# Carrying a scan's state in place, and moving table-switching work behind other exponentials, in a four-layer state-space kernel

## Chip, cores and metric

The kernel runs on one core of a Trainium2 chip. The metric is the device time of one execution in microseconds (us). The five engines are TensorE (PE; its weight loads are shown apart as PEld), VectorE (DVE), ScalarE (ACT), GpSimd (POOL) and SyncE (SP), which here issues the DMAs. The engines run beside each other, each one its own instructions in the order in which the program lists them, and wait for each other by semaphores.

## What is computed

Eight images of 48 x 48 pixels and 96 channels pass four layers, each with a group normalisation before it and a residual sum behind it. Layers 0 and 3 are two-dimensional selective scans, layer 2 scans rows and columns, and layer 1 is an up-sampled pointwise network. The three scan layers have the same core; layer 0's is this, cut down:

```python
xz = jnp.einsum('bhwc,ec->bhwe', x, in_proj_w)
xc, z = jnp.split(xz, 2, axis=-1)                     # 192 channels each
xc = jax.nn.silu(depthwise_conv_3x3(xc) + conv_b)
xs = jnp.stack([x0, x1, x0[..., ::-1], x1[..., ::-1]], axis=1)   # rows, columns, both reversed
dts, Bs, Cs = jnp.split(jnp.einsum('bkdl,kcd->bkcl', xs, x_proj_weight), [R, R + N], axis=2)
delta = jax.nn.softplus(jnp.einsum('bkrl,kdr->bkdl', dts, dt_projs_weight) + bias)
def step(h, inp):                                      # 2304 steps, N = 16 states a channel
    u, dl, Bv, Cv = inp
    h = h * jnp.exp(dl[..., None] * A) + (dl * u)[..., None] * Bv[:, :, None, :]
    return (h, jnp.einsum('bkdn,bkn->bkd', h, Cv))
...                                                    # + D * u, the four directions summed
y = layernorm(y) * jax.nn.silu(z)
return jnp.einsum('bhwd,cd->bhwc', y, out_proj_w)
```

In layers 0 and 3 the state runs through all 2304 pixels of an image. In layer 2 every row (or column) of 48 pixels begins with a state of zero.

## The kernel before

**Blocks, slots, turns.** `scans` treats the three scan layers alike. An image and direction is cut into five blocks of rows (`BLKS`): four of 480 pixels and one of 384. A block has 192 channels x 16 states; 128 partitions hold 32 channels x 4 states at a time, so that a block is 24 *units* of one row of 480 (or 384) columns. Three units make a *slot* (8 in a block), two slots a *turn* (4 in a block, `q` from 0 to 3). A layer has 160 blocks, so the kernel has 480.

**A unit's work.** ACT computes the decay, exp(A * delta), into PSUM (`make_da`, L255), two units at a time (*a pair*, three pairs in a turn; two buffers, `ps_da`). The product of delta * u (from the tile `dd`) and B is formed into the tile `dbu` (`make_dbu`, L235), some units by DVE and some by POOL: `ON_POOL` says how many of a slot's three units POOL takes. DVE reads B from a PSUM copy that ACT makes (`copy_b`, L216), POOL from the tile `bc`, which holds a row of B and a row of C. DVE scans a pair in place (`scan`, L263). POOL multiplies three units by C in place (`make_hc`, L276), and PE sums over the states (`reduce`, L296 and L298) and adds the result to the output in PSUM.

**The state between blocks.** In layers 0 and 3 a unit has one column more than the block has pixels (481 or 385). It holds the start state: the decay is zero there, because delta is set to `FAR` (1e30), and `dbu` holds the state. Behind the scan POOL copies the last column to a small tile (`keep`, L270), and ACT copies it into the start column of the same turn of the next block (`bring`, L243). In layer 2 (`restart`) there is no such column; `FAR` stands in every row's first pixel.

**Order.** Everything is written out by hand: within a turn, the loop at the end of `scans` lists pair 0's scan, the C product of the last turn's second slot, the B product of the next turn's first slot, pair 1's exponentials, and so on. `aside` is called twice in a turn, in the middle (an even half-turn, ahead of the next turn's first pair of exponentials) and at its end (an odd one, behind that pair, ahead of its second). There the DMAs of the next block are issued, a generator `side` advances by a step (the convolution of the next image and the output stage of the last one, in layers 0 and 3), and the steps of `stage1` run, which prepare the block after the next, each at its half-turn: projection (L611), copy (L616), delta (L601, L605), Softplus (L629), delta * u on POOL (`make_du`, L422) and the stores to DRAM, from where `dd` and `bc` are read back spread over the partitions.

**ACT's functions.** Exp, Softplus and Silu stand in different tables: each Softplus or Silu among the exponentials costs one table load before it and one behind it (rows ACT_TABLE_LOAD). In layers 0 and 3 Softplus stands at half-turn 6 and the convolution's two Silus (L491, L493) at 7. In layer 2 Silu of u (L747) stands at 6, Softplus (L775) at 8 and Silu of z (L789) at 10, which are 0 and 2 of the next block. Layer 2 also has, on DVE, a gated product (L803) and an addition to the image (L818, L820) behind a projection on PE (L812).

The main loop's middle, as an instance of the order:

```python
            scan(t, 1)
            make_da(t, 2)
            copy_b(at + 3)
            make_dbu(at + 3, nc.vector)
            if t > 0:
                reduce(t - 1, 1)
            aside(at)
            bring(t + 1)
            keep(t, 0)
            make_hc(t, 0)
            make_da(t + 1, 0)
            scan(t, 2)
            copy_b(at + 4)
            finish(at + 1)
            aside(at + 1)
```

Of the kernel before, what the change touches and what calls it, by code (L numbers as in the profile page):

```python
# [26 lines left out]
WMAX = BMAX + 1  # L27
# [12 lines left out]
ON_POOL = {1: 1, 3: 2, 5: 1, 7: 2}  # L40
# [18 lines left out]
class Block:  # L59


    def __init__(self, job, k, blk, first, last, rev):
        self.job, self.k, self.blk, self.first, self.last, self.rev = job, k, blk, first, last, rev
        self.r0, self.nr = BLKS[blk]
        self.n = self.nr * SEG

    def columns(self, restart):

        self.m = self.n + (0 if restart else 1)
        self.col = None if restart else self.n if self.rev else 0  # L70
        at = 0 if restart or self.rev else 1
        self.at = slice(at, at + self.n)
# [3 lines left out]
def vss_stack_kernel(ctx: ExitStack, tc: tile.TileContext, i: dict, out: bass.AP):  # L76
# [89 lines left out]
    def scans(dirs, order, restart, a, pools, ps, stage1, opening, done, side, tail):  # L166
# [7 lines left out]

        blocks = [Block(job, k, blk, n == 0, n == len(BLKS) - 1, dirs[k][1])
# [6 lines left out]
        carry = pools["carry"].tile([P, 24], F32, tag="carry", name="carry")  # L182
        zero = pools["carry"].tile([P, 6], F32, tag="zero", name="zero")
        nc.gpsimd.memset(zero, 0.0)
# [10 lines left out]
        def load_bc(t):  # L195
# [6 lines left out]
            r = pools["bc"].tile([P, 2 * BMAX], F32, tag=f"bc{n}", name=f"bc{n}")  # L202
            rows4 = b.bcd[8 * sg:8 * sg + 8, :].rearrange("(s w) n -> s (w n)", w=2)
            nc.sync.dma_start(r[:, :2 * b.n], rows4.unsqueeze(0).to_broadcast([32, 4, 2 * b.n]))
            bcs[t] = bcs[other] = r[:, :2 * b.n].rearrange("p (w n) -> p w n", w=2)

        def copy_b(t):
# [8 lines left out]
            nc.scalar.copy(bps[t][:, :b.n], bcs[t][:, 0, :b.n])  # L216
# [4 lines left out]
        def make_dbu(t, engine):  # L221
# [4 lines left out]
            if t // 2 not in dbus:  # L226
                dbus[t // 2] = pools["dbu"].tile([P, 6 * WMAX], F32, tag="dbu", name="dbu")
# [4 lines left out]
            o = units(dbus[t // 2], b, 3 * (slot % 2) + lo, 3 * (slot % 2) + hi)[:, :, b.at]  # L232
            du = b.got[ORDER[slot][0]][:, lo:hi, 1, b.at]
            by = bps[t][:, :b.n] if engine is nc.vector else bcs[t][:, 0, :b.n]
            engine.tensor_mul(o, du, by.unsqueeze(1).to_broadcast([P, hi - lo, b.n]))  # L235

        def bring(t):
# [4 lines left out]
            o = units(dbus[t], b, 0, 6)[:, :, b.col]  # L242
            nc.scalar.copy(o, zero if b.first else carry[:, 6 * q:6 * q + 6])  # L243
# [13 lines left out]
        def scan(t, pair):  # L257
# [3 lines left out]
            if b.rev:  # L261
                da, db = da[:, ::-1], db[:, ::-1]
            nc.vector.tensor_tensor_scan(db, da, db, 0.0, ALU.mult, ALU.add)  # L263

        def keep(t, sub):
            b, q = turns[t]
            if b.last or restart:
                return
# [861 lines left out]
```

## Time and profile before

| what | value |
|---|---|
| median of 3 runs | 19436.81 us (19431.89 to 19439.07) |
| the profiled execution: its own time | 19445.46 us |
| its span | 19443.7 us |
| DVE, POOL, PE, ACT busy | 16830.2, 16019.2, 15206.3, 14190.2 us |
| first scan layer, 130 to 5940 us: DVE, POOL busy | 5433.9, 5306.3 of 5810 us |
| pointwise layer, 5940 to 7373 us: DVE, POOL busy | 296.4, 20.2 of 1433 us |
| row layer, 7373 to 13490 us: DVE, POOL busy | 5624.9, 5356.0 of 6117 us |
| last scan layer, 13613 to 19426 us: DVE, POOL busy | 5433.9, 5306.5 of 5813 us |
| table loads on ACT, at L255 | 986 of 1283 ns each |
| DMA engines' mean busy share | 0.47 in the scan layers, 0.42 in the row layer |

The page gives, for each group of instructions, its line, engine, shapes and count, then its busy time and the mean duration of one, then the idle time of the engine just ahead of such instructions and what ended it. "<-ACT ps_da L255" behind an idle time means that the instruction started when ACT's line 255 had written `ps_da`. A group's mean mixes shapes where it says "+3 forms". In a timeline each row has its start, its duration, the engine and line, and in brackets the idle time ahead of it. Two neighbours' durations can overlap by some 0.08 us.

### The profile page before, as it was taken

What the parts mean: (1) busy time and instruction counts of PE and PEld (TensorE: products, weight loads), DVE (VectorE), ACT (ScalarE), POOL (GpSimd) and SP (SyncE); (2) the same over time, 40 slices, a digit from 0 to 9 for tenths busy, and PEclk for the clock granted to TensorE, in tenths of its full rate; (3) what the DMA queues carried; (4) which work ended last, traced back from release to release, by engine and by line L of the source; (5) the groups of instructions that cost most, each with busy time, mean ns of one, the idle gap of its engine ahead of it and who ended that gap; (6) DMA issues with size and microseconds to landing.
All of it is one profiled execution on the core that took longest, in us unless ns stands there. A gap on an engine that the chain in (4) does not pass through costs nothing.

```text
span 19443.7 us, 172969 instructions
## 1 busy us (share of the span) xinstructions
PE 15206.3 (78%) x53500; PEld 4384.0 (23%) x53500; DVE 16830.2 (87%) x11289; ACT 14190.2 (73%) x22262; POOL 16019.2 (82%) x9825
## 2 busy tenths in 40 slices
PE   6777777777777897888888988887777777777776
PEld 1211211211114562222222222222121121121121
DVE  7999999999993228999999999997999999999998
ACT  6777877877872227788788787786778778778776
POOL 6999999999991007888888888886999999999998
PEclk6776776776767777888888878878677677677675
DMA  4444444444443324444434444443444444444444
GB/s 135 162 159 162 160 159 162 159 161 161 156 165 60 49 43 147 145 142 151 149 141 147 147 143 146 147 145 119 158 162 159 160 162 160 157 162 161 157 162 138
DMA packets 768487, 2829.45 MB, mean 146 GB/s; under 512 B 235724, under 2 KB 298668, under 8 KB 640926
## 3 DMA queue, kind: packets, MB, share of 16 engines
q1 hardware_dynamic: 767558, 2818.38, 44.1%
q8 instruction: 422, 6.91, 0.1%
q14 instruction: 507, 4.15, 0.1%
HBM read 2371.42 MB, written 446.69 MB: 145 GB/s over the span
## 4 chain that ended last, share of the span: by engine, by line
DVE 32%; PE 19%; POOL 16%; ACT 15%; issue 13%; DMA 5%; SPq 0%; POOLq 0%; DVEq 0%; ACTq 0%
DVE dbu L263 20%; POOL dbu L276 12%; DVE dbu L235 11%; ACT ps_da L255 4%; PE ps_s L740 3%; ACT L255 3%; PE ps_y L296 3%; DMA dd<-dd 2%; PE ps_h L970 2%; POOL dds L422 2%; PE ps_s L611 2%; PE ps_y L983 2%; PE ps_s L812 1%; POOL dbu L235 1%; PE ps_side L482 1%
## 5 line engine op out<-in xcount | busy, mean ns | idle before, releaser
L263 DVE TENSOR_TENSOR_SCAN dbu<-ps_da,dbu 128x962 f32<-128x962 f32 (+3 forms) x5760 | 11853.3, 2070 | 927.4 <-ACT ps_da L255 925.1
L276 POOL TENSOR_TENSOR dbu<-dbu,bc 128x1440 f32<-128x1440 f32 (+1 forms) x3840 | 11433.5, 2984 | 1051.2 <-DVE dbu L263 837.5
L255 ACT ACTIVATE ps_da<-dd,w_l_a 128x481 f32<-128x481 f32 (+3 forms) x11520 | 7414.9, 648 | 2754.7 <-DVE dbu L263 2548.7
L296 PE MATMUL ps_y<-dbu,w_red 128*32 128x480 f32 (+1 forms) x23040 | 4947.0, 747 | 2996.0 <-POOL dbu L276 2991.6
L298 PE MATMUL ps_y<-dbu,w_red 128*32 128x480 f32 (+1 forms) x7680 | 4906.1, 747 | 0.0
L235 DVE TENSOR_TENSOR dbu<-dd,ps_b 128x1440 f32<-128x1440 f32 (+5 forms) x3840 | 4641.3, 1209 | 261.3 <-ACT ps_b L216 217.7
L235 POOL TENSOR_TENSOR dbu<-dd,bc 128x480 f32<-128x480 f32 (+3 forms) x1920 | 3023.4, 1575 | 58.8 <-DMA bc<-bcd 35.5
L296 PEld LDWEIGHTS ps_y<-dbu,w_red 128*32 128x32 f32 x23040 | 743.6, 125 | 6938.7 <-POOL dbu L276 5185.4
L216 ACT COPY ps_b<-bc 128x480 f32<-128x480 f32 (+1 forms) x3360 | 1798.8, 535 | 298.9 <-DVE dbu L235 270.1
L740 PE MATMUL ps_s<-xpad,w_l_cw 128*128 128x480 f32 (+1 forms) x2560 | 1760.7, 840 | 2.3 <-ACT xpad L124 1.6
L482 PE MATMUL ps_side<-xpad,w_l_cw 128*128 128x480 f32 (+1 forms) x2880 | 1652.6, 703 | 4.5 <-ACT xpad L124 4.5
L255 ACT ACT_TABLE_LOAD x986 | 1265.0, 1283 | 17.5
L113 POOL MEMSET w_l_cw<- 128x1760 f32 (+1 forms) x3 | 5.8, 1941 | 1346.3 <-DVE x L950 1340.9
L422 POOL TENSOR_TENSOR dds<-dds,u 96x480 f32<-96x480 f32 (+1 forms) x640 | 791.9, 1237 | 202.9 <-ACT dds L629 202.9
L601 PE MATMUL ps_s<-bcl,dtw 6*96 6x480 f32 (+1 forms) x1280 | 880.6, 777 | 90.7 <-ACT dds L605 80.9
L611 PE MATMUL ps_s<-u,w_l_xp 96*38 96x480 f32 (+1 forms) x1280 | 931.7, 867 | 2.8 <-ACT dds L605 1.5
L270 POOL COPY carry<-dbu 128x3 f32<-128x3 f32 x2048 | 382.5, 187 | 635.0 <-DVE dbu L263 628.5
L292 PE MATMUL ps_y<-ysum,w_ident 96*96 96x480 f32 (+1 forms) x960 | 747.5, 868 | 114.1 <-ACT ysum L652 112.6
L482 PEld LDWEIGHTS ps_side<-xpad,w_l_cw 128*128 128x128 f32 x2880 | 581.1, 227 | 1130.4 <-issue 940.9
L740 PEld LDWEIGHTS ps_s<-xpad,w_l_cw 128*128 128x128 f32 x2560 | 531.8, 213 | 1096.4 <-issue 961.9
L298 PEld LDWEIGHTS ps_y<-dbu,w_red 128*32 128x32 f32 x7680 | 683.1, 125 | 0.0
L768 PE MATMUL ps_s<-bcl,dtw 6*96 6x480 f32 (+1 forms) x640 | 424.1, 799 | 181.7 <-ACT bcl L762 181.7
(146 smaller groups left out, 12660.7 us busy)
## 6 DMA issues: line engine op xcount, KB each, us to landing
dd<-dd SPq DMA_DIRECT2D x512, 1443.0 KB
bc<-bcd SPq DMA_DIRECT2D x1536, 480.0 KB
dd<-dd SPq DMA_DIRECT2D x256, 1440.0 KB
dd<-dds SPq DMA_DIRECT2D x512, 360.8 KB
dd<-dd SPq DMA_DIRECT2D x128, 1155.0 KB
bc<-bcd SPq DMA_DIRECT2D x384, 384.0 KB
dd<-dds SPq DMA_DIRECT2D x256, 360.0 KB
dd<-dd SPq DMA_DIRECT2D x64, 1152.0 KB
```

Source lines behind the costliest of these rows:

```text
L216: nc.scalar.copy(bps[t][:, :b.n], bcs[t][:, 0, :b.n])
L235: engine.tensor_mul(o, du, by.unsqueeze(1).to_broadcast([P, hi - lo, b.n]))
L255: nc.scalar.activation(da[:, at:at + b.m], b.got[half][:, u % 3, 0, :], AF.Exp, scale=a[:, b.k, ci:ci + 1])
L263: nc.vector.tensor_tensor_scan(db, da, db, 0.0, ALU.mult, ALU.add)
L276: nc.gpsimd.tensor_mul(h, h, bcs.pop(2 * t + sub)[:, 1, :n].unsqueeze(1).to_broadcast([P, 3, n]))
L296: nc.tensor.matmul(y[32 * g:32 * g + 32, :n], lhsT=wc["red"][:, :32], rhs=hc[:, g, b.at], start=False, stop=(slot == 3))
L298: nc.tensor.matmul(y[DH:, :n], lhsT=wc["red"][:, 32:], rhs=hc[:, 2, b.at], start=(slot == 0), stop=(slot == 3))
L422: nc.gpsimd.tensor_mul(rows(du, n), rows(dt, n), u)
L482: nc.tensor.matmul(pu[:, :n], lhsT=flat[:, at:at + P], rhs=xpad[:, r0 + dy:r0 + dy + nr, dx:dx + W], start=(tap == 0), stop=(tap == 8))
L601: nc.tensor.matmul(got["p"][:DH, :n], lhsT=dtw[2 * NS:, b.k, half, :], rhs=b.bcl[2 * NS:, :n], start=True, stop=True)
L611: nc.tensor.matmul(got["p"][:NBC, :n], lhsT=w[f"{l}_xp"][:, b.k, half, :], rhs=u[:, half], start=(half == 0), stop=(half == 1))
L740: nc.tensor.matmul(got["u", half][:, :n], lhsT=flat[:, at:at + P], rhs=shifted(off), start=(tap == 0), stop=(tap == 3))
```

## The change

The unit of layers 0 and 3 grows to two extra columns, one at each end (482 or 386). `FAR` stands in the one where the scan comes in (`came`), zero in the other (`goes`), so that the scan itself copies its last state into the far column. The odd blocks of an image are held mirrored, and so are scanned in the other direction: the far column of one block is the start column of the next, and the four turns of a block have four fixed tiles (`rooms`), in which the state stays. `keep` and `bring` go. `begin` sets the start column to zero at an image's first block, and moves it where the block's length changes. The inputs and outputs of mirrored blocks are read and written through reversed views (`view`). The tile `bc` gets a leading column, so that B is read with its neighbours, and the rows of B and C start one column later.

POOL takes two units in slots 1, 5 and 7 and one in slot 3 (it was one in 1 and 5, two in 3 and 7): seven of a block's 24, where it was six.

In layers 0 and 3 Softplus moves from half-turn 6 to 7, both delta * u products stand at 8, and the convolution of the next image starts with a shorter first piece, so that its Silus fall on half-turn 3. In layer 2 the steps of `stage1` move one half-turn ahead, Silu to 5, Softplus to 7, Silu of z to 9; the copy of L762 stands apart from the matmuls ahead of it. In `aside` the steps behind a finished output (`later`) run ahead of `stage1`'s.

```diff
-WMAX = BMAX + 1
+WMAX = BMAX + 2
-ON_POOL = {1: 1, 3: 2, 5: 1, 7: 2}
+ON_POOL = {1: 2, 3: 1, 5: 2, 7: 2}
...
     def columns(self, restart):
-        self.m = self.n + (0 if restart else 1)
-        self.col = None if restart else self.n if self.rev else 0
-        at = 0 if restart or self.rev else 1
-        self.at = slice(at, at + self.n)
+        self.mirrored = not restart and self.blk % 2 == 1
+        self.back = self.rev != self.mirrored
+        if restart:
+            self.m = self.n
+            self.at = self.by = slice(0, self.n)
+            return
+        self.m = self.n + 2
+        self.at = slice(1, self.n + 1)
+        self.came, self.goes = (self.m - 1, 0) if self.back else (0, self.m - 1)
+        self.by = slice(0, self.n + 1) if self.back else slice(1, self.n + 2)
+
+    def view(self, t, col):
+        v = seq(t, col)
+        if len(v.shape) == 3:
+            v = v[:, self.r0:self.r0 + self.nr, :]
+            return v[:, ::-1, ::-1] if self.mirrored else v
+        v = v[:, :, self.r0:self.r0 + self.nr, :]
+        return v[:, :, ::-1, ::-1] if self.mirrored else v
...
-            nc.sync.dma_start(r[:, :2 * b.n], rows4.unsqueeze(0).to_broadcast([32, 4, 2 * b.n]))
+            nc.sync.dma_start(r[:, 1:1 + 2 * b.n], rows4.unsqueeze(0).to_broadcast([32, 4, 2 * b.n]))
+            lead = b.at.start
+            bcs[t] = bcs[other] = r[:, 1 - lead:1 - lead + b.m], r[:, 1 + b.n:1 + 2 * b.n]
...
-            nc.scalar.copy(bps[t][:, :b.n], bcs[t][:, 0, :b.n])
+            nc.scalar.copy(bps[t][:, :b.m], bcs[t][0])
...
-        def bring(t):
+        def begin(t):
             if t >= nt or restart:
                 return
             b, q = turns[t]
-            o = units(dbus[t], b, 0, 6)[:, :, b.col]
-            nc.scalar.copy(o, zero if b.first else carry[:, 6 * q:6 * q + 6])
+            o = units(rooms[q], b, 0, 6)[:, :, b.came]
+            if b.first:
+                nc.gpsimd.memset(o, 0.0)
+            elif blocks[t // (NG // 2) - 1].m != b.m:
+                c = blocks[t // (NG // 2) - 1]
+                nc.gpsimd.tensor_copy(o[:, 1:], units(rooms[q], c, 1, 6)[:, :, c.goes])
...
             next(beside, None)
-            run(at)
             for step in later.pop(at, []):
                 step()
+            run(at)
...
-            if b.rev:
+            if b.back:
                 da, db = da[:, ::-1], db[:, ::-1]
...
-                keep(t - 1, 1)
...
-            bring(t + 1)
-            keep(t, 0)
+            begin(t + 2)
...
-                        yield
+                        if not brief or slot in (2, 4, 6):
+                            yield
...
-            return {0: s0, 1: s1, 3: s3, 4: s4, 5: lambda: biased(1), 6: s6, 7: du(0), 8: du(1),
+            return {0: s0, 1: s1, 3: s3, 4: s4, 5: lambda: biased(1), 7: s6, 8: du,
                     NG + 1: store(0), NG + 2: store(1)}
...
-            return {3: conv(0), 4: conv(1), 6: s2s3, 7: s5, 8: s6, 9: s7, 10: s8, 11: lambda: store_dd(b, 1)}
+            return {2: conv(0), 3: conv(1), 5: s2, 6: s5, 7: s6, 8: s7, 9: s8, 10: lambda: store_dd(b, 1)}
```

## The prediction

> **What bounds the kernel now.** I read the page from the top: busy shares first, then the groups, then the waits, and last the timeline of one block, because the shares alone do not say which engine another engine's gain would reach.
>
> ```profile
> PE 15206.3 (78%) x53500; PEld 4384.0 (23%) x53500; DVE 16830.2 (87%) x11289; ACT 14190.2 (73%) x22262; POOL 16019.2 (82%) x9825
> ...
> L263 DVE TENSOR_TENSOR_SCAN dbu<-ps_da,dbu 128x962 f32<-128x962 f32 (+3 forms) x5760 | 11853.3, 2070 | 927.4 <-ACT ps_da L255 925.1
> L276 POOL TENSOR_TENSOR dbu<-dbu,bc 128x1440 f32<-128x1440 f32 (+1 forms) x3840 | 11433.5, 2984 | 1051.2 <-DVE dbu L263 837.5
> L270 POOL COPY carry<-dbu 128x3 f32<-128x3 f32 x2048 | 382.5, 187 | 635.0 <-DVE dbu L263 628.5
> ```
>
> DVE leads, POOL is close behind. The busy time by stretch says it more sharply: in the first scan layer (130 to 5940 us) DVE is busy 5433.9 of 5810 us and POOL 5306.3; in the row layer (7373 to 13490) 5624.9 and 5356.0 of 6117; the last scan layer repeats the first. The waits by engine say that POOL mostly waits for the scans (about 390 us in each scan layer, 666 in the row layer), and that DVE, where it is idle, mostly waits for exponentials: 310.9, 293.1 and 310.9 us in the three layers. So DVE sets the pace, and 925 us of its idle time have one releaser. The row layer has another 151 us of DVE waiting for PE (L820, L818, L803).
>
> The timelines of DVE and of ACT around one block border show where the 925 us arise.
>
> ```profile
> 3010.14 2.15 DVE L263 TENSOR_TENSOR_SCAN dbu<-ps_da,dbu 128x962 f32<-128x962 f32 x1
> 3012.83 2.16 DVE L263 TENSOR_TENSOR_SCAN dbu<-ps_da,dbu 128x962 f32<-128x962 f32 x1 [0.53 <-ACT ps_da L255]
> 3014.90 1.63 DVE L235 TENSOR_TENSOR dbu<-dd,ps_b 128x1440 f32<-128x1440 f32 x1
> 3018.25 2.16 DVE L263 TENSOR_TENSOR_SCAN dbu<-ps_da,dbu 128x962 f32<-128x962 f32 x1 [1.72 <-ACT ps_da L255]
> ...
> 3024.99 1.63 DVE L235 TENSOR_TENSOR dbu<-dd,ps_b 128x1440 f32<-128x1440 f32 x1
> 3026.54 2.15 DVE L263 TENSOR_TENSOR_SCAN dbu<-ps_da,dbu 128x962 f32<-128x962 f32 x1
> ```
>
> ```profile
> 3007.72 1.28 ACT L629 ACT_TABLE_LOAD   x1
> 3009.02 1.01 ACT L629 ACTIVATE dds<-dds 96x960 f32<-96x960 f32 x1
> 3009.93 0.18 ACT L243 COPY dbu<-zero 128x6 f32<-128x6 f32 x1
> 3010.13 1.28 ACT L255 ACT_TABLE_LOAD   x1
> 3011.43 1.37 ACT L255 ACTIVATE ps_da<-dd,w_l_a 128x481 f32<-128x481 f32 x2
> 3012.73 0.54 ACT L216 COPY ps_b<-bc 128x480 f32<-128x480 f32 x1
> 3013.29 1.28 ACT L491 ACT_TABLE_LOAD   x1
> ```
>
> The Softplus burst (3007.72 to 3011.43, two table loads) makes the next turn's first pair of exponentials 0.53 us late. The Silu burst of the convolution comes only one copy later, and makes the second pair 1.72 us late: ACT had no time to recover. I sorted the idle time before each of a block's 12 scans by its place. In a scan layer it is 107 us before scan 0 (Softplus), 135 before scan 1 (Silu, in about half of the blocks), 59 before scan 4, 12 elsewhere. In the row layer: 174 before scan 0 (Silu), 115 before scan 3 (Softplus), 8 elsewhere.
>
> **The change part by part.**
>
> 1. *Bursts behind the first pair.* A turn that nothing disturbs gives the slack. From the end of a turn's first scan, DVE needs 1.55 us (three-unit product, 3024.99 to 3026.54) + 2.07 (scan) + 0.54 or 1.05 (one- or two-unit product) + 2.07 until it wants the next turn's first pair, and 2.07 + 1.55 more until it wants the second. Before: ACT finishes its pair and copy 2.2 us after that point, a Softplus burst takes 3.71, a pair 1.36: ready at 7.3, wanted at 6.74, so 0.55 late, which the trace shows as 0.53. After: the first pair can start when scan 1 ends (3.62) and ends at 5.05, the copy at 5.6, the burst (3.5 without the copy of L243) at 9.1, the second pair at 10.5. It is wanted at 9.83, since the fourth turn now has the one-unit product. So Softplus still costs DVE about 0.7 us; by the same sum with the durations of the 384-column blocks (1.75 us a scan, 0.58 an exponential) 1.3. **The stall moves, it does not go**: 128 x 0.7 + 32 x 1.3 is about 130 us a layer, where it was 107. What goes is the collision: Silu now stands in the second turn by itself and costs the same 0.7 or 1.2, for 75 bursts (150 loads at L491 in two layers) about 60 us, where it was 135.
>
> 2. *Scan 4's wait* comes from the copy of L616, which waits for PE L611, which stands behind the reduction of POOL's last product of the block. The du product that stood ahead of that product on POOL (L422, 1.28 us) moves behind it, and the first turn's DVE product grows by a unit (0.5 us of slack). I take 59 down to 10 us; between 0 and 59. Per scan layer, then, 313 becomes 130 + 60 + 10 + 12 = 212, so -101, and -202 for both.
>
> 3. *Row layer.* All three bursts move to odd half-turns. Softplus (3.6 us) in the fourth turn: 130 us as above. Silu of u in the third turn has the gated product (0.6 us, L803) on DVE beside it: about 15. Silu of z in the first turn has that and a two-unit product: 0. With 8 elsewhere 153, where it was 297: -144. A new wait is added here: the Softplus load now comes half a turn after its matmuls of L768, not a full turn. They follow POOL's product and its reduction, ready by my sums about 1 us early; behind the load stand only exponentials, and DVE pays what comes late.
>
> 4. *One product unit in 24 goes from DVE to POOL.* DVE's rows by shape: 1129 ns for two units, 628 for one, 0.50 us a block; the short blocks 0.40. 384 x 0.50 + 96 x 0.40 = **231 us off DVE**, on the path while DVE is the bound. POOL pays 2.115 - 1.151 = 0.96 us a block by the same rows. Whether it can is the question of the next point. The "GPSIMD Engine Reference" of the Trainium skill (section Engine selection) speaks against this part: elementwise products belong on VectorE, GpSimd being about twice as slow. The rows agree on the price, 0.96 against 0.50. By that rule alone the kernel would lose 0.46 x 480, about 220 us; by the rows it wins as long as POOL keeps idle time.
>
> 5. *POOL's ledger.* The trace has a pattern: L276 takes 3.24 us in the row layer, but 2.90 or 3.07 in the scan layers, by the columns at which its three units start in their tile. A unit costs 1.08 where its own operand starts at column 0 or 1 modulo 4, and 0.91 at 2 or 3; this fits all shapes, and L422 and L235 too. After, two units lie 482 apart from column 1, so the scan layers get 2.90 and 3.07 alternately (now 3.07 throughout in the reversed directions), and their two-unit products of L235 become about 1.88, from 2.06. POOL's occupied time for an image, small gaps left out, is 666 us in a scan layer, DVE's 682, of 727. POOL after: about +6 (product units) - 6 (L276) + 2 (du) - 10 (the carry copies: 187 ns each, but the product behind follows so closely that only 0.08 us is won) + 2 = 660; DVE 673. Row layer: POOL 673 + 23 = 696, DVE 706 - 10 = 696. So POOL does not become the bound in the scan layers, and draws level in the row layer. But in all layers the rows of B and C now start at an odd column, which no row shows. If only the distance between the operands counts, the row layer's L276 drops to 2.73, 4 us a block off POOL; if odd starts cost all units the slow rate, it is 3.24 everywhere; the nearest row above that is L422 reading with a step, 1.44 for 480 columns. I take no effect, since odd starts of the other operand cost nothing extra.
>
> 6. *The rest.* The copies of L243 (1024 x 0.19 us) leave ACT, which has spare time; in the bursts they are counted above. Scans grow by two columns: by the slope between the 770 and 962 rows 4 ns, 3840 times, +16 us; the 960 and 962 rows differ by nothing, so 0 to 16. The few memsets and copies of the new start columns (512 on POOL, about 0.1 us) lie in POOL's spare time. Mirrored reads and writes have no row; contiguous and stepped rows (L652: 0.55 and 0.97, L611: 0.57 to 0.99) bound them, on engines with slack. In the row layer DVE's saved half microsecond in the second turn partly turns into waiting for the projection (L820 waits 74 times already): +40 us, between 0 and 77.
>
> Sum: -202 - 144 - 231 + 16 + 40 = **-521 us**. The profiled execution took 19445.46 us (span 19443.7), 8.7 above the median of 19436.81, so 18,924 by the profile's own time and about **18,915** as a median.
>
> The table loads deserve one more look. In the trace a load takes 1.28 us and the next instruction follows 0.02 us later. "ScalarE: Activation LUTs" of the Trainium skill (What ACT_TABLE_LOAD costs) adds a drain of about 1.4 us to each switch. By that page a burst would be some 2.8 us longer and this placement would stall DVE in every turn with a burst; the rows do not show the drain.
>
> **The rivals.**
>
> - *The bursts vanish altogether* (17%). For: POOL's and PE's lag shrink too, and a DVE slightly late at one place finds ACT ready at the next. Against: the slack sum above, which fits the old stall within 0.05 us. All remaining waits of 153 + 2 x 212 us gone gives 18,340; half of them 18,630. Range 18,350 to 18,750.
> - *Stalls only move, and POOL draws level everywhere* (13%): L276 at the slow rate in all layers. POOL's image in a scan layer is then 660 + 39 = 699, level with DVE and its stalls, and only point 4 is won, and partly: 19,437 - 231 + 56 = 19,260. Range 19,080 to 19,390.
> - *Slower* (12%): POOL becomes the bound because reading B and C from an odd column costs like a stepped read. POOL has 727 - 660 = 67 us an image to give, 19.2 full blocks with 8 products each: it decides from 0.43 us more per product, 3.4 us at L276. At 3.6 POOL needs 755 us an image in a scan layer, 28 more than now, 16 times, and 751 in the row layer, 15 fewer, 8 times: about 19,760. At 1.44 a unit (4.3 us) it would be above 21,500. For it: no row has this operand odd. Against: the other operand starts odd already without extra cost.
> - *It does not do what it says* (3%): within 0.2% of before. The order of the built program shows each burst directly behind a first pair and its copy, so this needs gains and losses to cancel.
>
> **How the numbers follow.** The forecast (18,760 to 19,080 by itself) has 55%. The 80% range runs from the middle of the first rival to the second's: 18,550 to 19,300. Faster by over 0.2% (39 us, about what a measurement here can tell from no change): 55 + 17 + 13 = 85%; within 0.2%: 3%; slower: 12%.
>
> **What would show it.** L263's wait for ACT falls from 925 to about 560 to 590 us, none of it before scan 0, most before scan 1; L235 on DVE loses 231 us, the same line on POOL gains at most some 400; carry lines are gone; L276's groups show 2.90 and 3.07 in the scan layers. Wrong would be: L276 above 3.4 us, DVE waiting for POOL at the scans, the gated products or the row layer's additions waiting longer for PE than 150 us more, or a scan wait above 800 us.

## The result, and the profile after

The changed kernel takes 19445.32 us (median of 12 runs, 19425.83 to 19452.23), the kernel before 19433.89 us beside it: a ratio of 1.0005, 95% interval 0.9996 to 1.0014. The forecast was 18,915 us. Nothing was won, although the copies are gone and the two busiest engines have less to do.

The page's engine line and the two costliest groups of the changed kernel (L289 is the scan, L295 the C product) stand against the first lines shown of before; carry copies no longer exist:

```profile
PE 15106.2 (78%) x53500; PEld 4344.8 (22%) x53500; DVE 16588.6 (85%) x11289; ACT 14003.6 (72%) x20977; POOL 15119.7 (78%) x8304
...
L289 DVE TENSOR_TENSOR_SCAN dbu<-ps_da,dbu 128x964 f32<-128x964 f32 (+3 forms) x5760 | 11820.8, 2069 | 846.0 <-ACT ps_da L281 844.6
L295 POOL TENSOR_TENSOR dbu<-dbu,bc 128x1440 f32<-128x1440 f32 (+1 forms) x3840 | 10670.3, 2796 | 2543.1 <-DVE dbu L289 2532.9 <-POOL dbu L295 0.4
```

DVE has 242 us less to do and POOL 900 us less, and the span is the same: both only wait more. The waits by engine of the changed kernel (in total, times, longest, in us) say where DVE does; L817 is the row layer's gated product:

```profile
DVE dbu L289 <- ACT ps_da L281: 844.6, 751, 4.2
DVE gated L817 <- PE ps_y L317: 499.7, 89, 8.9
...
DVE dbu L257 <- DMA dd<-dd: 83.9, 36, 4.4
```

The first was to fall to 560 to 590 us and has fallen by 81. The other two in before:

```profile
DVE dbu L235 <- DMA dd<-dd: 42.8, 29, 2.8
...
DVE gated L803 <- PE ps_y L298: 35.2, 56, 6.4
```

Two of the forecast's own signs of being wrong are there: the gated product waits 464 us longer for PE (the mark was 150), and a scan wait stands above 800 us.

From each trace I took the time between a layer's first scan and the first scan of its last block, which splits the zero into three parts. Kernels whose scan layers are alike (after, e1, e2, e3, e7) agree there within 8 us; from the first scan of scan layer 0's last block to the first of the row layer, mostly the pointwise layer, which no kernel changes, it is 1448 to 1483 us, so that small differences are better read by layer than in the total. The table has all kernels of this study; a ratio is to the runs of before on the same chip (their medians are 19,429 to 19,440 us):

| kernel | time, us | ratio to before, 95% interval | scan layer 0 | row layer | scan layer 3 |
|---|---|---|---|---|---|
| before | 19433.89 | 1 | 5771.4 | 6078.3 | 5774.5 |
| after | 19445.32 | 1.0005 [0.9996, 1.0014] | 5657.3 | 6313.9 | 5664.4 |
| e1_old_row_steps | 19098.01 | 0.9832 [0.9817, 0.9846] | 5659.0 | 5982.8 | 5660.7 |
| e2_conv1_back | 19375.44 | 0.9975 [0.9965, 0.9984] | 5662.5 | 6245.1 | 5657.7 |
| e3_softplus_back | 19513.91 | 1.0044 [1.0030, 1.0059] | 5655.2 | 6392.2 | 5658.8 |
| e4_units_back | 19464.63 | 1.0017 [1.0007, 1.0026] | 5680.3 | 6286.5 | 5681.3 |
| e5_scan_bursts_only | 19350.98 | 0.9952 [0.9937, 0.9966] | 5729.1 | 6073.2 | 5726.2 |
| e6_in_place_only | 19244.77 | 0.9900 [0.9885, 0.9915] | 5725.1 | 5984.6 | 5726.6 |
| e7_conv_by_rows | 19117.85 | 0.9832 [0.9813, 0.9852] | 5660.0 | 5983.2 | 5661.9 |
| e8_units_by_layer | 19079.15 | 0.9811 [0.9794, 0.9827] | 5649.6 | 5954.3 | 5648.7 |
| e9_bc_one_later | 19373.60 | 0.9968 [0.9956, 0.9981] | 5785.5 | 5997.7 | 5783.2 |
| e10_bc_three_later | 19392.74 | 0.9977 [0.9967, 0.9986] | 5749.1 | 6070.7 | 5750.1 |
| e11_second_dds | 19451.38 | 1.0008 [0.9999, 1.0017] | 5783.0 | 6082.3 | 5787.4 |
| e12_best_second_dds | 19167.00 | 0.9865 [0.9852, 0.9879] | 5700.3 | 5952.8 | 5702.4 |

The scan layers won 114 and 110 us, the row layer lost 236. The forecast had about -170 for each scan layer and -180 for the row layer, so the miss is first of all there.

**The stall in the row layer.** A block of the changed kernel in a column direction, in the timelines of DVE, PE and POOL:

```profile
10122.38 2.17 DVE L289 TENSOR_TENSOR_SCAN dbu<-ps_da,dbu 128x960 f32<-128x960 f32 x1
10128.66 0.65 DVE L817 TENSOR_TENSOR gated<-zb,ps_y 96x480 f32<-96x480 f32 x1 [4.11 <-PE ps_y L317]
```

```profile
10112.33 2.50 PE L826 MATMUL ps_s<-gated,wo 96*96 96x480 f32 x4
10114.67 12.18 PE L763 MATMUL ps_s<-xpad,w_l_cw 128*128 128x384 f32 x16
10126.78 0.60 PE L315 MATMUL ps_y<-dbu,w_red 128*32 128x480 f32 x3
```

```profile
10112.83 5.42 POOL L295 TENSOR_TENSOR dbu<-dbu,bc 128x1440 f32<-128x1440 f32 x2 [1.64 <-DVE dbu L289]
```

POOL had both C products of a turn done at 10118.25. Their reductions (L315, L317) stand in PE's queue behind the convolution of the block after the next (L763, 16 records in one piece, 12.18 us), and begin at 10126.78. The gated product waits for the last of them, DVE 4.11 us. This convolution is of a block of 384 pixels; for 480 pixels the 16 records take 15.18 us. For 384 pixels in a row direction they take 5.33 us, and DVE does not wait:

```profile
9719.60 5.33 PE L763 MATMUL ps_s<-xpad,w_l_cw 128*128 128x384 f32 x16
```

In the row layer's old order, half-turns 3 and 4, the two reductions stand between the convolution's halves; in the new, 2 and 3, nothing does.

A second stall comes with Softplus. ACT, DVE and PE of the changed kernel, around the new place of Softplus (L789):

```profile
9697.93 0.54 ACT L238 COPY ps_b<-bc 128x480 f32<-128x480 f32 x1
9701.76 1.28 ACT L789 ACT_TABLE_LOAD   x1 [3.29 <-issue]
9703.06 1.20 ACT L789 ACTIVATE dds<-ps_s,w_l_dtb 96x480 f32<-96x480 f32 x2
9704.28 1.28 ACT L281 ACT_TABLE_LOAD   x1
9705.58 2.64 ACT L281 ACTIVATE ps_da<-dd,w_l_a 128x480 f32<-128x480 f32 x4
```

```profile
9701.17 1.63 DVE L257 TENSOR_TENSOR dbu<-dd,ps_b 128x1440 f32<-128x1440 f32 x1
9706.97 2.16 DVE L289 TENSOR_TENSOR_SCAN dbu<-ps_da,dbu 128x960 f32<-128x960 f32 x1 [4.17 <-ACT ps_da L281]
```

```profile
9699.78 3.51 PE L782 MATMUL ps_s<-bcl,dtw 6*96 6x480 f32 x4
```

ACT stands 3.29 us in front of the load, in the trace under "issue", that is without a releaser. That it waits for the matmuls that Softplus reads (L782, begun at 9699.78) is inferred from the times. Idle ahead of scan 1 is 1.80 us a block on average, 286 us for the layer; that of ACT ahead of these loads is 124.2 us (62 of the 160 wait, up to 3.3 us).

### The profile page after: what moved, and what is told of

The parts are those of the page before. It is cut to its first block, busy times and chain, and to the rows that moved or that the text cites. A ratio compares the mean times of both kernels' runs of the same rounds, so it can differ in the third digit from the quotient of the medians.

```text
span 19446.5 us, 169763 instructions
## 1 busy us (share of the span) xinstructions
PE 15106.2 (78%) x53500; PEld 4344.8 (22%) x53500; DVE 16588.6 (85%) x11289; ACT 14003.6 (72%) x20977; POOL 15119.7 (78%) x8304
## 4 chain that ended last, share of the span: by engine, by line
DVE 34%; PE 23%; ACT 19%; issue 14%; DMA 6%; POOL 4%; SPq 0%; DVEq 0%; ACTq 0%; POOLq 0%
DVE dbu L289 22%; DVE dbu L257 10%; ACT ps_da L281 6%; PE ps_s L763 6%; PE ps_y L315 4%; ACT L281 4%; POOL dbu L295 3%; DMA dd<-dds 2%; PE ps_h L984 2%; PE ps_y L311 2%; ACT ps_b L238 2%; PE ps_y L997 2%; PE ps_side L502 1%; ACT L651 1%; DMA dd<-dd 1%
## 5 line engine op out<-in xcount | busy, mean ns | idle before, releaser
L295 POOL TENSOR_TENSOR dbu<-dbu,bc 128x1440 f32<-128x1440 f32 (+1 forms) x3840 | 10670.3, 2796 | 2543.1 <-DVE dbu L289 2532.9
L289 DVE TENSOR_TENSOR_SCAN dbu<-ps_da,dbu 128x964 f32<-128x964 f32 (+3 forms) x5760 | 11820.8, 2069 | 846.0 <-ACT ps_da L281 844.6
L281 ACT ACTIVATE ps_da<-dd,w_l_a 128x482 f32<-128x482 f32 (+3 forms) x11520 | 7391.9, 648 | 2920.0 <-DVE dbu L289 2701.0
L315 PE MATMUL ps_y<-dbu,w_red 128*32 128x480 f32 (+1 forms) x23040 | 5091.0, 776 | 2019.3 <-POOL dbu L295 2016.5
L317 PE MATMUL ps_y<-dbu,w_red 128*32 128x480 f32 (+1 forms) x7680 | 5051.9, 776 | 0.0
L257 DVE TENSOR_TENSOR dbu<-dd,ps_b 128x1443 f32<-128x1443 f32 (+10 forms) x3840 | 4410.2, 1148 | 307.3 <-ACT ps_b L238 218.9
L257 POOL TENSOR_TENSOR dbu<-dd,bc 128x962 f32<-128x962 f32 (+6 forms) x1920 | 3104.4, 1617 | 105.3 <-DMA bc<-bcd 72.3
L315 PEld LDWEIGHTS ps_y<-dbu,w_red 128*32 128x32 f32 x23040 | 811.9, 130 | 6081.6 <-POOL dbu L295 4353.9
L238 ACT COPY ps_b<-bc 128x482 f32<-128x482 f32 (+3 forms) x3360 | 1793.0, 534 | 248.6 <-DVE dbu L257 214.9
L763 PE MATMUL ps_s<-xpad,w_l_cw 128*128 128x480 f32 (+1 forms) x2560 | 1683.6, 819 | 7.5 <-DVE x L834 5.4
L623 PE MATMUL ps_s<-bcl,dtw 6*96 6x480 f32 (+1 forms) x1280 | 945.1, 830 | 753.3 <-ACT z L515 557.0
L311 PE MATMUL ps_y<-ub,diag 96*96 96x480 f32 (+1 forms) x640 | 513.9, 900 | 499.6 <-DVE gated L817 499.6
L763 PEld LDWEIGHTS ps_s<-xpad,w_l_cw 128*128 128x128 f32 x2560 | 512.5, 201 | 1075.8 <-issue 971.3
L317 PEld LDWEIGHTS ps_y<-dbu,w_red 128*32 128x32 f32 x7680 | 749.3, 131 | 0.0
L817 DVE TENSOR_TENSOR gated<-zb,ps_y 96x480 f32<-96x480 f32 (+1 forms) x320 | 195.3, 610 | 499.7 <-PE ps_y L317 499.7
```

Source lines behind the costliest of these rows:

```text
L238: nc.scalar.copy(bps[t][:, :b.m], bcs[t][0])
L281: nc.scalar.activation(da[:, at:at + b.m], b.got[half][:, u % 3, 0, :], AF.Exp, scale=a[:, b.k, ci:ci + 1])
L295: nc.gpsimd.tensor_mul(h, h, bcs.pop(2 * t + sub)[1].unsqueeze(1).to_broadcast([P, 3, n]))
L311: nc.tensor.matmul(ys[b, half][:DH, :n], lhsT=lhsT, rhs=rhs, start=True, stop=False)
L315: nc.tensor.matmul(y[32 * g:32 * g + 32, :n], lhsT=wc["red"][:, :32], rhs=hc[:, g, b.at], start=False, stop=(slot == 3))
L317: nc.tensor.matmul(y[DH:, :n], lhsT=wc["red"][:, 32:], rhs=hc[:, 2, b.at], start=(slot == 0), stop=(slot == 3))
```

## Experiments

First the theory: the row layer's steps cost what the rest wins, because PE's queue is in their way. Its rivals: the unit that went to POOL, the odd column, or mirrored reads cost it.

**e1, the row layer's steps put back**, all else as changed.

```diff
+            run(at)
             for step in later.pop(at, []):
                 step()
-            run(at)
...
-            return {2: conv(0), 3: conv(1), 5: s2, 6: s5, 7: s6, 8: s7, 9: s8, 10: lambda: store_dd(b, 1)}
+            return {3: conv(0), 4: conv(1), 6: s2, 7: s5, 8: s6, 9: s7, 10: s8, 11: lambda: store_dd(b, 1)}
...
-                for _ in range(3 * NG + 3):
+                for _ in range(3 * NG + 4):
```

> The changed kernel with the row layer's steps back at their old half-turns (convolution 3 and 4, Silu 6, Softplus 8, Silu of z 10, and the steps behind a finished output after them); all else stays changed. Theory A: the row layer lost 236 us by its moved steps alone: the convolution's eight matmuls now stand ahead of two reductions in PE's queue (the gated product waits 500 us for PE, where it was 35), and Softplus stands too close behind its matmuls. Then the gated wait returns to about 35 us, the row layer takes 6030 to 6080 us instead of about 6310, and the kernel about 19,150 to 19,200. Theory B: PE was already the hidden bound of the row layer, and what DVE saves there comes back as waits for PE whatever the steps: then the row layer stays above 6200 us and the kernel above 19,350.

19098.01 us, below what was expected: the row layer loses 331 us, the scan layers stay. So the moved steps alone cost 331 us, where -144 were forecast, and the unit, the odd column and the mirrored reads, which e1 keeps, do not cost it. Its waits:

```profile
DVE dbu L289 <- ACT ps_da L281: 837.7, 822, 3.6
DVE gated L817 <- PE ps_y L317: 25.3, 27, 5.4
```

**e2, only the convolution's second half put back** to half-turn 4, so that the reductions pass between.

```diff
-            return {2: conv(0), 3: conv(1), 5: s2, ...
+            return {2: conv(0), 4: conv(1), 5: s2, ...
```

> The changed kernel with only the second half of the row layer's convolution back at half-turn 4, so that it stands behind the reductions of the turn's first half in PE's queue. Theory A: the gated wait for PE falls from 500 us to under 100, Silu of u waits for PE by 1 to 3 us in the 80 column blocks instead, and about 200 to 350 us of the kernel's time go: 19,100 to 19,250. Theory B (PE is the bound anyway): the gated wait falls, but the same time comes back in the waits before the scans, and the kernel stays within 60 us of 19,445.

```profile
DVE dbu L289 <- ACT ps_da L281: 1256.6, 832, 7.4
```

The gated wait is gone (21.1 us), but only 69 us of time in the row layer, where 200 to 350 were expected; the whole lies between the ranges of the two theories. Silu of u at half-turn 5 (L770) now waits 421.7 us for the convolution's end (267.3 in the changed kernel), with the exponentials behind it, and idle ahead of scan 10 goes from 0.19 to 2.97 us a block. One queue was relieved, the next has the same matmuls in its way.

**e3, only Softplus put back** to half-turn 8, with Silu of z still at 9.

```diff
-            return {..., 7: s6, 8: s7, 9: s8, ...
+            return {..., 8: lambda: (s6(), s7()), 9: s8, ...
...
-                for _ in range(3 * NG + 3):
+                for _ in range(3 * NG + 1):
```

> The changed kernel with only the row layer's Softplus back at half-turn 8, ahead of Silu of z at 9 (the normalisation of the next image starts two half-turns earlier, which its PSUM buffer needs). Theory A: the 286 us of waiting before a block's second scan go, since Softplus no longer follows its own matmuls; but Silu of z comes one copy behind it, the collision that the scan layers had before: 0.5 us before scan 3 and up to 1.7 before scan 4, 100 to 300 us in 160 blocks. The gated wait of 500 us stays. So 19,350 to 19,450. Theory B: no wait for Softplus's matmuls was in it, the 286 us are the burst's own length, and they stay or only change their place: 19,440 to 19,550.

Idle ahead of scan 1 is gone, as theory A said, but 1.41 us a block stand ahead of scan 4, where two bursts now follow each other, and the gated wait grows to 567.8 us. The row layer is 78 us longer, so the time lies in theory B's range: the waiting mostly changed its place.

**e7, the convolution reads by rows in all directions**, order as changed. In the column directions that is another input than the layer's: e7 leaves out the transposed reading and serves to measure alone.

```diff
-                                         rhs=shifted(off), start=(tap == 0), stop=(tap == 3))
+                                         rhs=flatly(off), start=(tap == 0), stop=(tap == 3))
```

> The changed kernel, but the row layer's convolution reads the image by rows in the two column directions as well (another input for these directions; all else as in the changed kernel). Theory A: what stands ahead of the reductions is the length of the eight matmuls when they read down a column, about 12 us where they take 5 in the row directions: the gated product's wait for PE falls from 500 us to under 60, and the row layer from about 6310 to about 5900, the kernel to about 19,000 to 19,100. Theory B: the order on PE alone is at fault, whatever the length: the gated wait stays above 200 us.

```profile
DVE dbu L289 <- ACT ps_da L281: 1009.7, 834, 4.2
DVE gated L820 <- PE ps_y L317: 7.6, 10, 5.4
```

The convolution's records in after, then in e7:

```profile
L763 PE MATMUL ps_s<-xpad,w_l_cw 128*128 128x480 f32 (+1 forms) x2560 | 1683.6, 819 | 7.5 <-DVE x L834 5.4 <-ACT xpad L142 1.6 <-ACT zb L803 0.5
```

```profile
L766 PE MATMUL ps_s<-xpad,w_l_cw 128*128 128x480 f32 (+1 forms) x2560 | 1028.5, 551 | 9.9 <-DVE x L837 6.9 <-ACT xpad L142 1.6 <-ACT zb L806 0.7
```

With the order untouched and only the duration of the same matmuls changed (a mean of 551 ns for 819), the gated wait goes and the row layer loses 331 us. e1 keeps the length and changes the order, e7 the reverse, and the gated wait goes in both: the long form at this place in PE's queue is its cause. That both win the same time is partly chance, for e7 still has Softplus coming late (2.56 us a block ahead of scan 1, where e1 has none). The kernel's 19117.85 us lie just above the expected range.

**e4, POOL's units put back**, all else as changed.

```diff
-ON_POOL = {1: 2, 3: 1, 5: 2, 7: 2}
+ON_POOL = {1: 1, 3: 2, 5: 1, 7: 2}
```

> The changed kernel with POOL's share of the products as before (one unit in slots 1 and 5, two in 3 and 7). Theory A: DVE is the bound in both scan layers and gets 0.5 us a block back: +77 us in each; in the row layer, where DVE waits for PE at the gated product, most of it is hidden: 0 to +77. So 19,600 to 19,680. Theory B: POOL or PE bounds the scan layers now, and the kernel stays within 60 us of 19,445.

The unit is worth 23 and 17 us in the scan layers, and minus 27 in the row layer with its new steps; 77 each were forecast. The time lies in theory B's range, but not for its reason: in the first scan layer of the changed kernel POOL waits 457 us for scans. Occupied time of DVE for an image of a scan layer goes from 673 back to 683 us, but its idle time falls from 38 to 30. By place, idle ahead of scan 1 is 0.43 us a block with the old units and 0.75 with the new, ahead of scan 7 0.24 and 0.46: the work was taken out of the turns in which a burst of ACT needs cover.

**e5 and e6, single parts on the kernel before.** e5 has the scan layers' moved bursts alone (conv's shorter first piece, Softplus at 7, both du at 8), e6 the state in place alone, with its tiles and the leading column of `bc`.

> The kernel before with one part of the change: in the two scan layers Softplus at half-turn 7, both delta * u products at 8, the convolution's Silus at 3. States, units and row layer as before. Theory A: it is this part that won the scan layers' time, since the two bursts of one block border no longer collide: each scan layer loses 50 to 90 us of its 5771 (first scan of the first block to the first scan of the last), so 19,260 to 19,340. Theory B: the scan layers' gain of 114 us each comes from the unit moved to POOL and from the copies that went, and the bursts only change their place: 19,400 to 19,450.

> The changed kernel with all steps and POOL's share of the units as before: only the states are carried in place. Theory A: the copies were hidden on POOL and ACT, so that alone this part wins little: ACT's 0.2 us in each Softplus burst, 0 to 30 us a scan layer; nothing in the row layer although POOL's products there fall from 3.24 to 2.73 us, as POOL does not bound it. 19,370 to 19,440. Theory B: POOL's shorter queue (carry copies gone, product 0.5 us shorter in the row layer) shortens what PE and DVE wait for: 19,250 to 19,350.

The bursts are worth 42 and 48 us in the scan layers, a little less than the 50 to 90 expected. The state in place is worth 46 and 48 there (0 to 30 expected), and, unforeseen, 94 us in the row layer, in which no state is carried. For a scan layer the three parts give 42 + 46 + 23 = 111, and 114 were measured. In the row layer -94 and the +331 of the steps give 237, and 236 were measured.

In e5, idle ahead of scans falls by 81 us a layer. A part returns as a wait that before did not have in this layer: DVE waits 49 us for `dd`. Over all layers, in the waits of e5:

```profile
ACT dds L607 <- DMA dd<-dds: 202.1, 125, 14.1
...
DVE dbu L235 <- DMA dd<-dd: 133.8, 120, 4.3
```

It was 31.3 and 42.8 us. The stores of `dds` now stand on SP's queue waiting for the later Softplus (1742.4 us in e5, 363.0 in before), and the loads behind them start later.

**e9 and e10: the kernel before, with B and C one or three columns later** in the tile `bc`.

```diff
-            r = pools["bc"].tile([P, 2 * BMAX], F32, tag=f"bc{n}", name=f"bc{n}")
+            r = pools["bc"].tile([P, 1 + 2 * BMAX], F32, tag=f"bc{n}", name=f"bc{n}")
...
-            nc.sync.dma_start(r[:, :2 * b.n], rows4.unsqueeze(0).to_broadcast([32, 4, 2 * b.n]))
+            nc.sync.dma_start(r[:, 1:1 + 2 * b.n], rows4.unsqueeze(0).to_broadcast([32, 4, 2 * b.n]))
```

> The kernel before with one edit: the rows of B and C start at column 1 of the tile bc, not at 0, in all layers. Distance theory: what a unit of a POOL product costs hangs on how far its two operands' start columns lie apart, modulo 4 (0.91 us at 2 or 3, 1.08 at 0 or 1). Then L276 takes 2.73 us in the row layer (now 3.24), and in the scan layers 3.07 in three of four cases and 2.90 in one, as now but in other blocks; the row layer loses about the 94 us that the kernel with the in-place state alone lost there, from 6078 to about 5985, the scan layers stay at 5771 within 10, and the whole is about 19,340 us, 0.995. Rival, the fixed tiles for the scans or the memsets brought the 94 us in that kernel: L276 may change, but the row layer stays within 20 us of 6078, ratio 1.000. Rival, any odd column costs: L276 slower somewhere and the time above 1.000.

> The same edit with column 3 in place of 1. Distance theory: in the row layer the operands lie 1 apart modulo 4, so L276 stays at 3.24 us and the row layer at 6078 within 15; in the scan layers L276 takes 2.90 us in three of four cases and 3.07 in one (now the reverse), 0.68 us a block off POOL, which by the row layer's rate (94 us of time for 640 of POOL) is about 15 us a layer; the whole about 19,405 us, 0.998 to 0.999. Rival, an odd start of B and C is what makes it fast: L276 takes 2.73 us in the row layer as with column 1, and the row layer loses some 90 us.

L276 within the row layer (7450 to 13300 us), by shape, of before, of e9 and of e10 (busy, mean in ns, idle):

```profile
L276 POOL TENSOR_TENSOR dbu<-dbu,bc 128x1440 f32<-128x1440 f32 x975 | 3146.6, 3243 | 504.5 <-DVE dbu L263 459.7 <-DMA bc<-bcd 44.2
```

```profile
L276 POOL TENSOR_TENSOR dbu<-dbu,bc 128x1440 f32<-128x1440 f32 x985 | 2688.7, 2735 | 1041.4 <-DVE dbu L263 973.4 <-DMA bc<-bcd 68.0
```

```profile
L276 POOL TENSOR_TENSOR dbu<-dbu,bc 128x1440 f32<-128x1440 f32 x970 | 3132.6, 3245 | 494.0 <-DVE dbu L263 457.2 <-DMA bc<-bcd 36.1
```

One column makes the product 0.51 us shorter, three columns do nothing: it is the distance, not the odd start, and not the fixed tiles, which e9 does not have. The scan layers answer too: their full products take 3.07, 3.07, 3.07 and 2.91 us in e9, 2.91, 2.90, 3.08 and 2.91 in e10, each of the eight as the distances say. In time, e9 wins 81 us in the row layer, of the 94 of e6, and loses 14 and 9 in the scan layers, which I had at 0 within 10; e10 wins 22 and 24 there.

**e8, the fastest: e1 with POOL's units chosen by layer**, three of them in slot 7, so that DVE and the copy of B skip it.

```diff
-ON_POOL = {1: 2, 3: 1, 5: 2, 7: 2}
+ON_POOL = {False: {1: 1, 3: 2, 5: 1, 7: 3}, True: {1: 1, 3: 1, 5: 2, 7: 3}}
...
+            if ON_POOL[restart].get(slot) == 3:
+                return
```

> The changed kernel with the row layer's old steps, and seven units a block on POOL as in the change, but in other slots: those whose turn has no burst give a unit, those with a burst keep it on DVE, where it is the slack that hides part of the burst (scan layers: one unit of slots 1 and 5, two of 3, three of 7; row layer: one of 1 and 3, two of 5, three of 7). Theory A: a unit taken from DVE in a turn with a burst wins nothing, since DVE then waits as much longer for the exponentials; in a turn without, it wins its 0.5 us. So the scan layers lose another 50 us each and the row layer 80 against 19,098: 18,880 to 18,960. Theory B: a unit's place does not matter, only DVE's total: 19,070 to 19,130.

19079.15 us, 9 and 12 us less than e1 in the scan layers and 28 in the row layer, with as many units on POOL. It beats both kernels; beside e1 the intervals overlap. Idle ahead of scan 1 is 0.44 us a block in the scan layers, for e1's 0.75, so the place decides where DVE waits. In time theory A failed by its sizes (50 and 80 us), and the whole lies in theory B's range: of the 51 us less of waiting ahead of scans in the first scan layer, 12 come back as waiting for `dd` and 25 as busy time of DVE itself, whose cause stays open.

**e11 and e12, a second buffer for `dds`**, in e5 and in e8. The room came from the output stage: two small tiles share a buffer, the input tile `xi` has one for two.

```diff
-                 "carry": pool("carry", 1), "dds": pool("dds", 1), "bcl": pool("bcl", 1),
+                 "carry": pool("carry", 1), "dds": pool("dds", dds), "bcl": pool("bcl", 1),
...
-        wt, big, zp, lnp, xio = pool("wt", 1), pool("big", 3), pool("z", 1), pool("ln", 2), pool("xio", 2)
+        wt, big, zp, lnp, xio = pool("wt", 1), pool("big", 3), pool("z", 1), pool("ln", 2), pool("xio", 1)
```

> The kernel before with the scan layers' bursts moved alone (19,350.98 us; its scan layers 5729.1 and 5726.2 us, idle ahead of scan 7 about 0.33 us a block, ScalarE's line 607 waiting 202 us for the store of dds) and, in layers 0 and 3, a second buffer for the tile dds; to make room, two small tiles of the output stage share a buffer and its input tile has one buffer instead of two. Theory: behind the moved steps the store of dds starts later, so ScalarE's next write to dds waits for it to land, with the exponentials queued behind. Then that wait goes to near 0, the idle ahead of scan 7 falls below 0.1, each scan layer loses 30 to 45 us (about 5690), and the whole is about 19,270 us; VectorE's wait for dd (134 us) stays, since the store and the load behind it are as late as before. Rival: the idle ahead of scan 7 is the Silu burst itself, moved; then the wait for dds goes and the scan layers stay at 5729 within 10 us. Rival: the shared tiles of the output stage cost as much as the second buffer wins; then the waits of the lines behind xi and sq grow by 30 us or more a layer.

> The same second buffer for dds in the fastest kernel so far (the changed kernel with the row layer's old steps and POOL's units chosen by layer: 19,079.15 us, scan layers 5649.6 and 5648.7). Theory of the store: idle ahead of scan 7 (0.24 us a block) and part of that ahead of scan 4 go, each scan layer 20 to 40 us shorter, the whole about 19,020 us, 0.978 to 0.980 of before. Rival, the Silu burst itself: 19,079 within 15 us.

My theory fell. ACT's wait for the store of `dds` is gone, yet idle ahead of scan 7 stays (0.32 us in e11, 0.33 in e5): that is the Silu burst, in its new place. Ahead of scan 9 it falls from 0.20 to 0.06, so that was the store. And each scan layer becomes longer, by 54 and 61 us in e11, 51 and 54 in e12: with one buffer the load of `xi` waits on SP's queue for the store of the last, with the loads of `dd` behind it. That was the second rival. SP's waits in the first scan layer of e11, then DVE's in all layers:

```profile
SPq L535 <- DMA x<-xi: 164.1, 28, 10.2
```

```profile
DVE dbu L235 <- DMA dd<-dd: 280.1, 121, 9.9
```

The second buffer's own worth is left open: no kernel here has it beside two of `xi`.

## Why the prediction was wrong, point by point

The sum of the forecast beside what single parts were worth: bursts in the scan layers (points 1 and 2) -202, measured -90; the row layer's steps (3) -144, measured +331; the unit (4) -231, measured -40 in the scan layers and -2 in the row layer with its old steps; the state in place (6) +16, measured -188, of which 94 in the row layer; DVE's waiting for the projection (6) +40, gone in the changed kernel. That is +11 for -521.

- **Point 3 is the step that failed**: the row layer, -144 forecast, +331 measured (after against e1). It costed the bursts that move and the Softplus matmuls, and left out what else moves: the convolution's 16 records on PE, which at half-turns 2 and 3 stand in one piece ahead of two reductions. Half of the directions read down the columns and need 12.18 to 15.18 us there. This gave the gated wait of 499.7 us, and e7 shows that it is the convolution's length. The second part, "ready by my sums about 1 us early", was wrong in sign: 62 of the 160 loads wait, up to 3.3 us, 124.2 us in all, and idle ahead of scan 1 is 286 us for the 130 of the sum. What point 3 had right: the bursts ahead of scans 0 and 3 are gone (0.02 and 0.00 us a block for 1.09 and 0.72), and the row additions' wait for PE fell from 116 to 2 us, where point 6 feared 40 more.
- **Point 1** was right in mechanism, and for the waits nearly in size. A Softplus burst behind the first pair of the changed kernel, in ACT's and DVE's timelines:

```profile
3030.26 1.28 ACT L651 ACT_TABLE_LOAD   x1
3031.56 1.01 ACT L651 ACTIVATE dds<-dds 96x960 f32<-96x960 f32 x1
3032.58 1.28 ACT L281 ACT_TABLE_LOAD   x1
```

```profile
3033.10 1.62 DVE L257 TENSOR_TENSOR dbu<-dd,ps_b 128x1443 f32<-128x1443 f32 x1
3035.28 2.17 DVE L289 TENSOR_TENSOR_SCAN dbu<-ps_da,dbu 128x964 f32<-128x964 f32 x1 [0.56 <-ACT ps_da L281]
```

  The second pair is 0.56 us late for the 0.7 of the sum (here a step of the output stage stands ahead of the burst on ACT and one on DVE); the layer's mean ahead of scan 1 is 0.75, 120 us for 130. Silu, ahead of scan 7, costs 0.46, 73 us for 60. As in before, no drain stands behind a load.
- **Point 2**: 59 us ahead of scan 4 were to fall to 10 and fell to 39. The copy behind the projection still waits for PE (L638, 2.69 us at 3042.01). With point 1, a layer's idle ahead of scans was to be 212 us and is 258. Beside this came DVE's wait for `dd`, 43 us in the first scan layer: the moved stores on SP, which the sum had not followed, as it had not followed the convolution on PE.
- **Point 4**: 231 us were taken off DVE (its busy time falls by 242), but moving the unit alone wins only 40 in the scan layers and nothing in the row layer (e6 and e1, 5984.6 and 5982.8). The step that failed is to count the 231 as a gain "on the path while DVE is the bound". In the turns with a burst ACT ends last, and DVE's products are its cover: the pair is wanted half a microsecond earlier, and DVE waits for it. Point 1 had this ("wanted at 9.83, since the fourth turn now has the one-unit product") and put it into the 130 us, but the forecast never asked what of the 231 was left by its own sums. The "GPSIMD Engine Reference" of the Trainium skill (section Engine selection) would keep such products on VectorE. The runs do not settle for or against it: from e4 to after, moving the unit wins 40 us in the scan layers and loses 27 in the row layer.
- **Point 5**: POOL did not become the bound. Of the two cases named for the odd column, I took neither, and the first is true: only the distance counts, the C product is 2.73 us in the row layer, and e9 shows 81 us for it. Occupied, POOL has 596 us for an image there, where the sum had 696. The carry copies were priced too low at 0.08 us: in the trace of before the product behind a copy starts 0.27 us after the copy does (the median of 2048), and in e6 POOL's occupied time for an image of a scan layer, small gaps counted in, is 633 us for 677.
- **Point 6** held in its first part: the scans' extra columns cost nothing that shows (a mean of 2069 ns, 2070 before).
- **The rivals.** "Slower" by reads at an odd column is excluded by e9. The time fell on the case with 3%, gains and losses that cancel. It is the coincidence that this case names: a loss of 331 us that I had not priced meets gains of about 320, of which 188 were not priced either. That they cancel to 11 us is chance.

Without the row layer's steps the same change is worth 331 us beside its own runs of before (e1, 0.9832, 0.9817 to 0.9846), nearly two thirds of the 521 forecast for the whole, but not for the reasons given: 188 us of it come from the state in place, which the sum had at +16.

## What to carry to other kernels

When a step moves, list its instructions on every engine, and for each queue say what comes to stand behind it; the longest form counts (here the column reads), not the mean. Work taken off the leading engine is won in full only in turns where nothing else ends last: here 40 us were won of 154 in the scan layers, and the rest came back as waiting where the work had covered a burst. Before a long elementwise product on POOL is moved or split, try the start columns of its operands.

## What the runs showed of the hardware

- A POOL product of two inputs takes 1.03 us for 480 columns when the start column of its own operand (also the output's) minus that of the other is 2 or 3 modulo 4, and 1.21 us at 0 or 1. Products of three units follow it in all of before, after, e9 and e10: 2.73 us (all at 3), 2.90, 3.07 and 3.24 us (all at 0 or at 1). e9 and e10 differ in nothing but this column. A product of one unit in the row layer, in before (distance 0) and in after (3):

```profile
L235 POOL TENSOR_TENSOR dbu<-dd,bc 128x480 f32<-128x480 f32 x243 | 294.0, 1210 | 20.9 <-DMA dd<-dd 13.9 <-PE ps_y L298 3.7 <-issue 3.2
```

```profile
L257 POOL TENSOR_TENSOR dbu<-dd,bc 128x480 f32<-128x480 f32 x119 | 123.1, 1035 | 0.0
```

- The same matmul costs more when it reads down the columns: the row layer's convolution took 819 ns a record in the changed kernel (half of the blocks by columns; granted clock 0.80 in that layer) and 551 ns in e7 (none; 0.78). "SBUF — State Buffer" of the Trainium skill (section Door 1, its note on cachelines of 16 bytes) says that each access which crosses to a new line pays a penalty; the direction agrees, and a size it does not give.
- A DMA that waits holds up the DMAs behind it on SP's queue: in e11, beside e5, the load of `xi` waits 164.1 us for a store in the first scan layer, and DVE's wait for `dd` more than doubles, from 133.8 to 280.1 us over all layers.
